# Four-layer graph network on one core: another order in layer 1's sort, table loop and last pass, and other places for chunk loads

## The chip, the core and the metric

The kernel runs on one core of one Trainium2 chip. The core's engines are TensorE (PE, matrix products into PSUM; the loading of its weights is shown apart as PEld), VectorE (DVE), ScalarE (ACT) and GpSimd (POOL). Data move between DRAM and the on-chip memory by DMA. Here the queue of SyncE (SP) issues the plain loads and stores, POOL's queue issues the indirect ones (gathers and scatters by row number), and a few come from ACT's queue. Each queue runs in order.

The metric is the device time of one execution in microseconds (us). Before the change it is 1217.2 us, the median of three runs (1211.95, 1217.2, 1225.6).

## The reference, cut to what matters

`x` is 2708 x 128 and `adj` is 2708 x 2708, both float32. Four layers run one after the other, each on `h = max(layernorm(x), 0)` with a residual sum. The change touches layer 1 and the aggregation that ends it:

```python
def _L1_gnn_ref(X, A, W, a):
    XW = jnp.matmul(X, W)
    s_col = jnp.matmul(XW, a[0, :f])
    s_row = jnp.matmul(XW, a[0, f:])
    Z1 = jax.nn.leaky_relu(s_row[:, None] + s_col[None, :], negative_slope=0.01)
    den = jnp.exp(Z1)
    num = jnp.matmul(A, den)
    att = jnp.where(num != 0, den / jnp.where(num != 0, num, 1.0), 0.0)
    H = jnp.matmul(A, jnp.matmul(att, XW))
    return H
...
h = jnp.maximum(_layernorm(x, axis=-1), 0.0)
x = x + _L1_gnn_ref(h, adj, L1_gnn_W, L1_gnn_a)
```

Layers 0, 2 and 3 each need a product of the whole of `adj` with 128 features as well; layer 0 also needs the four nearest neighbours of every node.

## The kernel before, in words

`adj` comes in transposed, so row k of it in DRAM is column k of `A`. It is cut into T = 22 **chunks** of 128 rows (1.354 MB each); the last chunk, number 21, has only 20 rows. The 2708 columns are cut into six blocks of at most 512, one PSUM bank each (`acc(0)` to `acc(5)`; two more banks, `ps_s`, serve short products in turn). On chip, chunks lie in `big` (four buffers), in five or six `res` buffers, or, for two of them, in the `lay` buffers with tags "Y" and "U", which other large tiles use at other times.

**Layer 1 without the big product.** `num` would be a 2708 x 2708 x 2708 product. But exp(leaky_relu(s_row + s_col)) is one of two products of exponentials, and which one holds for node k and column j depends only on whether s_row[k] lies above -s_col[j]. So the kernel sorts the nodes by s_row, builds a table with one row for each place in the sorted order (a *knot*), and finds every column of `num` by interpolating between two neighbouring rows of it. The stages are:

- *Sort (lines 748 to 883).* For t = 0 to 21, `place(t)` compares all nodes with the 128 of tile t: a mask on DVE (L779), its sum on ACT (L780), and counts on PE (L757). After every fourth tile `places_of` (L788) turns the counts into sorted places: a copy on DVE (L793), small products on PE (L797), `to_u` on DVE (L809), and then one scatter for each tile from POOL's queue (L814), which writes node number and s_row to `order_d` in DRAM. In between, `total(x_)` (L839) multiplies one chunk after the other, in 16 small products on PE (L847), into `tot`, the weighted total of all rows. Nine chunks are on chip already (`here`); thirteen more are loaded on SP's queue by `total_chunk` (L826, L836). The thirteen, n = 0 to 12, go to "Y", "U", then the four `big` buffers, and from n = 6 on to the five row buffers in turn. `total` is called at t = 1 to 11 and at even t from 12, one chunk a time, and what is left after the loop. `node_terms` (L857, a few small operations on PE, DVE and ACT for the columns' own terms) runs at t = 14.
- *Start of the table (L938 to L1005).* The sorted list is read back (`srtT`, L938), transposed on PE and turned into row numbers `src_u` (L943) and values `rs` (L944). `fetch(t)` (L946) gathers 126 rows of `adj` in sorted order into a `big` buffer (L950). The totals are moved into row 1 of the first of these tiles (L966, two DMAs from ACT's queue and two from SP's). Then `wt`, a 128 x 128 triangle of weights for every tile, is made: 44 matmul instructions on PE in six groups into `acc(1)` to `acc(5)` (L988), and 22 Relu operations on ACT (L999).
- *Table loop (L1030 to L1052).* For t = 0 to 21: the gather for t + 3 is issued, six products `wt[t]` x rows (L1036) give 128 knots, rows 0 and 1 are carried into the next tile on DVE (L1040), the knots are copied out on ACT and DVE (L1041) and stored to the table in DRAM on SP's queue (L1050, L1052). ACT also forms one row of signs (L908) a turn, four tiles ahead; `row_places` (L1016), at t = 19, finds from the signs which two table rows each column needs (`lo_u`, `hi_u`). Every third turn holds a group of XW (`node_product`, L1047).
- *Last pass (L1149 to L1158).* For each of the 22 tiles of 128 columns: gather the rows `lo` and `hi` (L1073), seven operations on single columns (L1094 to L1104), the interpolation on DVE (L1119), Ln and Exp on ACT (L1123, L1124), the product with `den` on DVE (L1131), and six products with XW on PE that add up in `py` (L1141). Tiles 0 to 3 are handled one by one and the others in pairs (`sets`); tile t is weighted (L1131, L1141) after tile t + 1 is interpolated. Tiles 0, 20 and 21 are split into two halves (`parts_of`). `lo` has four buffers, those of `big`; `hi` has six.
- *Aggregation (`aggregate`, L256).* `H` = A x (att XW): chunks 0 to 15 pass through the four `big` buffers, and chunks 16 to 21 are loaded into `res` buffers that stay for layers 2 and 3. In program order the load of `res` chunk 16 + i // 2 stands after chunk i for odd i: 0, 1, 16, 2, 3, 17, and so on. Chunk 21 is loaded four times, to four groups of 20 partitions. `aggregate` does the products of chunks 0 to 15 first, those of 16 to 21 at the end, and `res` buffers exist only once the last pass has left its `hi` buffers.

Program order sets the order of instructions marked `pin` only; the others on an engine may be moved by the scheduler that builds the program.

## Time and profile before

The profiled execution took 1218.29 us by its own clock; its span, from first to last instruction, is 1216.2 us, at a mean granted TensorE clock of 0.928. Stage by stage, from the busy time of each engine in stretches of the span:

| stretch, us | what runs | PE busy | DVE busy | ACT busy | POOL busy | DMA, GB/s |
|---|---|---|---|---|---|---|
| 484 to 537 | sort, totals | 46.86 | 33.46 | 36.24 | 24.20 | 290 |
| 537 to 700 | weights, table loop | 130.92 | 100.39 | 102.50 | 23.11 | 356 |
| 700 to 728 | start of last pass | 0.00 | 10.08 | 9.19 | 10.02 | 342 |
| 728 to 865 | last pass | 102.98 | 129.48 | 105.06 | 81.47 | 389 |
| 865 to 888 | its end, evacuation | 22.43 | 15.30 | 7.14 | 0.00 | 85 |
| 888 to 970 | aggregation, chunks 0 to 15 | 76.88 | 1.19 | 0.00 | 1.62 | 357 |
| 970 to 1000 | its end, next layer's start | 30.00 | 13.28 | 10.12 | 0.00 | 55 |

The stretches before 484 us are layer 0, those after 1000 us layers 2 and 3. A busy engine need not be the one that sets the pace, and an engine can be on the path while it is little busy; which wait ends last in each stretch has to be read from the single instructions. In the timeline each line has the start and the length in us, the engine, the line of the program, the operation with its operands, the number of merged instructions, and in brackets how long the engine had been idle before it and what it then waited for.

### The profile page before, as it was taken

What the parts mean: (1) busy time and instruction counts of PE and PEld (TensorE: products, weight loads), DVE (VectorE), ACT (ScalarE), POOL (GpSimd) and SP (SyncE); (2) the same over time, 40 slices, a digit from 0 to 9 for tenths busy, and PEclk for the clock granted to TensorE, in tenths of its full rate; (3) what the DMA queues carried; (4) which work ended last, traced back from release to release, by engine and by line L of the source; (5) the groups of instructions that cost most, each with busy time, mean ns of one, the idle gap of its engine ahead of it and who ended that gap; (6) DMA issues with size and microseconds to landing.
All of it is one profiled execution on the core that took longest, in us unless ns stands there. A gap on an engine that the chain in (4) does not pass through costs nothing.

```text
span 1216.2 us, 10253 instructions
## 1 busy us (share of the span) xinstructions
PE 1054.7 (87%) x3637; PEld 507.0 (42%) x3637; DVE 563.8 (46%) x1172; ACT 407.5 (34%) x643; POOL 237.0 (19%) x200
## 2 busy tenths in 40 slices
PE   4889999999969996977787807777999999999998
PEld 0325444444424445543333303333454455545444
DVE  2001004899972357816666648999720040114003
ACT  3100003444430034767667436878600040003000
POOL 0200000000017773441111035866000000000000
PEclk8998999999989996978989857998889999999999
DMA  8997830000059823869999889999299807753831
GB/s 307 426 359 299 307 133 1 1 0 1 1 218 400 318 53 113 360 222 322 367 380 403 350 351 418 424 424 380 82 383 351 317 33 276 268 184 105 308 136 46
DMA packets 40160, 298.77 MB, mean 246 GB/s; under 512 B 7103, under 2 KB 11214, under 8 KB 13650
## 3 DMA queue, kind: packets, MB, share of 16 engines
q1 hardware_dynamic: 24076, 202.37, 44.3%
q0 software_dynamic: 13600, 93.75, 20.3%
q10 hardware_dynamic: 2434, 2.01, 0.6%
q8 instruction: 29, 0.48, 0.2%
q14 instruction: 21, 0.17, 0.0%
HBM read 265.76 MB, written 32.87 MB: 246 GB/s over the span
## 4 chain that ended last, share of the span: by engine, by line
PE 53%; DVE 20%; DMA 19%; issue 6%; POOL 1%; ACT 1%; SPq 0%; POOLq 0%; DVEq 0%; ACTq 0%
PE acc L267 40%; DMA mov<-in_adj_dram,src_u 7%; DVE top_v L474 5%; DMA chunk<-in_adj_dram 5%; DVE top_i L476 5%; DVE hi L1131 4%; DVE hi L1119 4%; DMA hi<-table,hi_u 2%; DMA res<-in_adj_dram 2%; PE ps L847 2%; PE acc L1036 2%; PE acc L1141 1%; PE ps L224 1%; DMA xs<-in_x_dram 1%; PE ps L355 1%
## 5 line engine op out<-in xcount | busy, mean ns | idle before, releaser
L1141 PE MATMUL acc<-hi,xw 128*128 128x512 f32 (+2 forms) x264 | 119.8, 612 | 63.2 <-DVE hi L1131 63.2
L267 PE MATMUL acc<-chunk,y 128*128 128x512 f32 (+1 forms) x408 | 159.3, 554 | 12.8 <-DVE y L518 10.7
L267 PE MATMUL acc<-chunk,h 128*128 128x512 f32 (+1 forms) x384 | 148.0, 542 | 0.0
L1036 PE MATMUL acc<-mov,wt 128*128 128x512 f32 (+1 forms) x264 | 119.7, 608 | 28.7 <-DMA mov<-in_adj_dram,src_u 28.7
L539 POOL DMA_INDIRECT gath<-ydr,near_u x88 | 84.4, 959 | 284.8 <-DMA ydr<-y 258.3
L267 PEld LDWEIGHTS acc<-chunk,y 128*128 128x128 f32 x408 | 75.0, 194 | 97.1 <-issue 85.6
L463 PE MATMUL acc<-zT 128*128 128x512 f32 (+2 forms) x264 | 108.2, 552 | 1.5 <-ACT strip L472 1.1
L1141 PEld LDWEIGHTS acc<-hi,xw 128*128 128x128 f32 (+1 forms) x264 | 53.7, 212 | 129.1 <-DVE hi L1131 66.7
L1040 DVE COPY mov<-acc 2x512 f32<-2x512 f32 (+1 forms) x126 | 74.6, 612 | 61.0 <-PE acc L1036 59.6
L267 PEld LDWEIGHTS acc<-chunk,h 128*128 128x128 f32 x384 | 68.8, 190 | 74.1 <-issue 74.1
L1036 PEld LDWEIGHTS acc<-mov,wt 128*128 128x128 f32 x264 | 52.5, 210 | 92.0 <-issue 78.0
L472 ACT COPY strip<-acc 128x512 f32<-128x512 f32 (+2 forms) x132 | 60.7, 558 | 73.5 <-issue 58.5
L267 PE MATMUL acc<-chunk,attended 128*128 128x512 f32 x192 | 76.9, 563 | 5.1 <-DMA chunk<-in_adj_dram 5.1
L463 PEld LDWEIGHTS acc<-zT 128*128 128x128 f32 (+1 forms) x264 | 46.4, 185 | 57.3 <-issue 34.1
L1073 POOL DMA_INDIRECT lo<-table,lo_u x22 | 56.0, 2547 | 71.5 <-DVE hi L1119 31.5
L1041 ACT COPY knots<-acc 128x512 f32<-128x512 f32 x88 | 49.9, 586 | 55.7 <-DVE mov L1040 40.0
L1119 DVE SCALAR_TENSOR_TENSOR hi<-lo,lam,hi 128x2708 f32<-128x2708 f32 (+4 forms) x25 | 67.2, 2697 | 1.0
L1123 ACT ACTIVATE hi<-hi,lam 128x2708 f32<-128x2708 f32 (+4 forms) x25 | 56.7, 2280 | 32.5 <-issue 23.4
L1131 DVE SCALAR_TENSOR_TENSOR hi<-row_all,inv_s,hi 128x2708 f32<-128x2708 f32 (+4 forms) x25 | 67.0, 2692 | 0.0
L474 DVE MAX8 top_v<-strip 128x8 f32<-128x2708 f32 (+1 forms) x22 | 64.3, 2963 | 0.2 <-ACT strip L472 0.2
L476 DVE FIND_INDEX8 top_i<-top_v,strip 128x8 uint32<-128x2708 f32 x20 | 59.2, 2972 | 0.0
L545 DVE SCALAR_TENSOR_TENSOR xs<-gath,simd,xs 128x128 f32<-128x128 f32 (+1 forms) x88 | 30.6, 351 | 59.9 <-DMA gath<-ydr,near_u 59.2
(270 smaller groups left out, 1168.1 us busy)
## 6 DMA issues: line engine op xcount, KB each, us to landing
chunk<-in_adj_dram SPq DMA_DIRECT2D x110, 1354.0 KB
table<-knots SPq DMA_DIRECT2D x20, 1354.5 KB
res<-in_adj_dram SPq DMA_DIRECT2D x9, 1354.0 KB
res<-in_adj_dram SPq DMA_DIRECT2D x8, 211.6 KB
ydr<-y SPq DMA_DIRECT2D x2, 704.0 KB
gath<-ydr,near_u POOLq DMA_INDIRECT x88, 5.5
chunkY<-in_adj_dram SPq DMA_DIRECT2D x1, 1354.0 KB
chunkU<-in_adj_dram SPq DMA_DIRECT2D x1, 1354.0 KB
```

The costliest lines, as they stand in the source:

```text
L267: nc.tensor.matmul(out[b][:, :n], y[r, i, :], chunk(i)[r, k0 : k0 + n], start=(i == 0), stop=(i == T - 2),)
L463: mm = nc.tensor.matmul(zz[b][:w, :n], zT[:, cols(t)], zT[:, k0 : k0 + n], start=True, stop=False)
L472: nc.scalar.copy(s[:w, k0 : k0 + n], zz[b][:w, :n])
L474: nc.vector.max(top_v[:w, t, :], s[:w, :])
L476: nc.vector.max_index(top_i[:w, t, :], top_v[:w, t, :], s[:w, :])
L539: nc.gpsimd.indirect_dma_start(out=g[:w, :], out_offset=None, in_=ydr[:, :], in_offset=bass.IndirectOffsetOnAxis(ap=near_u[:w, t, k : k + ...
L1036: nc.tensor.matmul(p[:, :n], wt[:, t, :], moving[t][:, k0 : k0 + n], start=True, stop=True)
L1040: nc.vector.tensor_copy(moving[t + 1][:2, k0 : k0 + n], p[:2, :n])
L1119: nc.vector.scalar_tensor_tensor(num, lo[:w, c], kap, num, op0=ALU.mult, op1=ALU.add)
L1123: nc.scalar.activation(num, num, AF.Ln, scale=sc)
L1131: nc.vector.scalar_tensor_tensor(att[:w, c], row_all[:w, c], inv_s[:w, t : t + 1], att[:w, c], op0=ALU.max, op1=ALU.mult,)
L1141: nc.tensor.matmul(py[b][:, :n], xw[:w, t, :], att[:w, k0 : k0 + n], start=(t == 0), stop=(t == T - 1),)
```

## The change

There are five parts. (1) *Sort:* the last two chunk loads, n = 11 and 12, go to "U" and "Y" instead of the row buffers; `total` is called at t = 1 to 13 and at 15, 16, 18 and 20; `node_terms` runs at t = 16. (2) *Start of the table:* the first three gathers are issued right after `src_u`, ahead of `rs` and the totals; the four DMAs of the totals all go on SP's queue. (3) *Table loop:* the weights are made in groups of four tiles, the first before the loop and group t // 4 + 1 at the end of turn t for t = 0, 4, 8, 12, 16, in the `ps_s` banks; `row_places` runs at t = 18. (4) *Last pass:* tile 21, the one of 20 columns, is first, alone and not split; then 0, 1, 2 alone, and the pairs (3, 4) to (19, 20). (5) *Aggregation of layer 1:* `back=3` puts the loads of the `res` chunks two chunks later: 0, 1, 2, 3, 16, 4, 5, 17, and so on, with 21 after 13. The other aggregations keep their order (`back=1`).

```diff
-    def aggregate(y, done, more=None, kept=0):
+    def aggregate(y, done, more=None, kept=0, back=1):
...
-            if i % 2 and last + i // 2 < T:
-                chunk(last + i // 2)
+            j = last + (i - back) // 2
+            if i >= back and (i - back) % 2 == 0 and j < T:
+                chunk(j)
...
-        if n < 2:
-            c = lay.tile([P, N], F32, name="chunk" + "YU"[n], tag="YU"[n])
+        if n < 2 or n > 10:
+            tag = "YU"[n % 2]
+            c = lay.tile([P, N], F32, name="chunk" + tag, tag=tag)
...
-        if t == 14:
+        if t == 16:
             node_terms()
-        if 1 <= t <= len(here) + 2 or t % 2 == 0 and t:
+        if 1 <= t <= len(here) + 4 or t in (15, 16, 18, 20):
             total(done)
...
     nc.vector.tensor_copy(src_u[:PER, :], p[:PER, :T])
-    nc.vector.tensor_copy(rs, p[:, T : 2 * T])
...
+    for t in range(3):
+        fetch(t)
+    nc.vector.tensor_copy(rs, p[:, T : 2 * T])
...
-        (nc.scalar, nc.sync)[g % 2].dma_start(
+        nc.sync.dma_start(
             first[1:2, QUARTER * g : QUARTER * (g + 1)], tots[32 * g : 32 * g + 1, :]
         )
-    for t in range(3):
-        fetch(t)
...
-    for t0, t1 in GROUPS:
-        p = acc(1 + t0 // 4 % 5)
+
+    def weights(g):
+        t0, t1 = GROUPS[g]
+        p = ps_s.tile([P, 512], F32, name="ps")
...
+
+    weights(0)
...
-        if t == T - 3:
+        if t == T - 4:
             row_places()
+        if t % 4 == 0 and t // 4 + 1 < NG:
+            weights(t // 4 + 1)
...
-        return [slice(0, HALF), slice(HALF, N)] if t < 1 or t >= T - 2 else [slice(0, N)]
+        return [slice(0, HALF), slice(HALF, N)] if t in (0, T - 2) else [slice(0, N)]
...
-                start=(t == 0),
-                stop=(t == T - 1),
-            )
-
-    sets = [(t,) for t in range(4)] + [(t, t + 1) for t in range(4, T, 2)]
+                start=(t == T - 1),
+                stop=(t == T - 2),
+            )
+
+
+    sets = [(T - 1,)] + [(t,) for t in range(3)] + [(t, t + 1) for t in range(3, T - 1, 2)]
...
-            if t:
-                weighed(t - 1)
-    weighed(T - 1)
+            if before:
+                weighed(before.pop())
+            before.append(t)
+    weighed(before.pop())
...
-    aggregate(attended, to_h2, ahead(lambda g: node_product(yT, None, g, attend), 1))
+    aggregate(attended, to_h2, ahead(lambda g: node_product(yT, None, g, attend), 1), back=3)
```

## The prediction

> **What bounds the kernel now.** I read the chain of waits first: no engine bounds the whole span, so I took layer 1 stage by stage, from the timeline of each engine and the busy time in stretches. There are four places where something other than the busiest engine ends a wait.

> *The end of the sort.* First the chain of waits, then POOL's timeline:

> ```profile
> 525.49 8.28 DMA chunk<-in_adj_dram
> 533.82 2.48 PE ps L847 x16
> ```
> ```profile
> 528.23 0.89 POOL L814 DMA_INDIRECT order_d<-pay,to_u  x1 [0.30 <-issue]
> 534.25 0.59 POOL L938 DMA_DIRECT2D srtT<-order_d  x1 [5.14 <-DMA order_d<-pay,to_u]
> 537.81 1.10 POOL L950 DMA_INDIRECT mov<-in_adj_dram,src_u  x1 [2.97 <-DVE pw L979]
> ```

> Two strands end together near 536: the last chunk, issued at 525.49 only because a row buffer came free late, and the last scatter, for which POOL idles 5.14. The first gather starts at 537.81.

> *The table loop.* PE's timeline:

> ```profile
> 552.37 4.78 PE L1036 MATMUL acc<-mov,wt 128*128 128x512 f32 x12 [1.36 <-DMA mov<-in_adj_dram,src_u]
> 559.31 6.48 PE L1036 MATMUL acc<-mov,wt 128*128 128x512 f32 x12 [2.16 <-DMA mov<-in_adj_dram,src_u]
> ...
> 694.08 4.78 PE L1036 MATMUL acc<-mov,wt 128*128 128x512 f32 x12 [0.90 <-DMA mov<-in_adj_dram,src_u]
> ```

> Turns 1, 2 and 21 start when their gathers land: (694.08 - 552.37) / 20 = 7.09 a gather. The first interval is 6.94, most of it before the first table store at 554.35: the stream of gathers sets the pace, not PE, ACT or the stores.

> *The start of the last pass.* DVE's timeline:

> ```profile
> 716.46 0.21 DVE L1094 TENSOR_SCALAR lam<-hi,lo 128x1 f32<-128x1 f32 x1 [3.25 <-DMA hi<-table,hi_u]
> ...
> 749.50 0.21 DVE L1094 TENSOR_SCALAR lam<-hi,lo 128x1 f32<-128x1 f32 x1 [3.08 <-DMA hi<-table,hi_u]
> ...
> 750.75 3.04 DVE L1119 SCALAR_TENSOR_TENSOR hi<-lo,lam,hi 128x2708 f32<-128x2708 f32 x1
> ```

> `hi` of tile 0 lands at 716.4, of tile 5 at 749.4: 6.6 a tile, so the stream began at 709.8. From 750.75 DVE has no gap to the end; a pair takes 13.39 (777.74 - 764.35).

> *The aggregation.* PE's timeline:

> ```profile
> 888.04 51.98 PE L267 MATMUL acc<-chunk,attended 128*128 128x512 f32 x132
> 942.32 6.51 PE L267 MATMUL acc<-chunk,attended 128*128 128x512 f32 x12 [2.29 <-DMA chunk<-in_adj_dram]
> 951.65 18.44 PE L267 MATMUL acc<-chunk,attended 128*128 128x512 f32 x48 [2.83 <-DMA chunk<-in_adj_dram]
> ```

> PE waits twice for chunks. From 970 to 1180 it is busy without a gap, so what is won before arrives at the end in full.

> [...] while chunk 21's four 20-row loads were in flight (934 to 942) the engines moved 135 to 184 GB/s, against some 420 otherwise. [...] the read of the sorted list took 2.0, the quickest scatter 2.1.

> **Part 1 and 2, sort and start.** "U" and "Y" are free by 509.9 (the last product that reads U), so loads 11 and 12 are issued near 510 instead of 523.27 and 525.49. The nine before them fill the DMA until about 520.9; two at 3.2 (1.354 MB at 420 GB/s) end near 527.3, not 531.6, and the last totals near 532 instead of 536.3. Then the scatters decide. Up to `places_of(3)` the count of totals stays thirteen and `node_terms` is gone (about 1.0 of PE; its DVE operations add up to 1.6): tiles 12 to 15 may go about 1 sooner. From there to `places_of(4)` PE gains one total (16 products, 1.25) and `node_terms` (1.0). So `to_u` of tiles 16 to 19, at 520.78 now, comes 0.5 to 2.4 later; POOL, which reaches them at 521.87, is held about 0.9. Six scatters of 1.27 follow: the last starts near 529.1. Beside a quiet DMA it needs 2.1 to 2.6, not 5.4: the sorted list is read at about 531.9, 2.3 sooner. The gather now waits for `src_u` (done at 536.90) and not for DVE work to 537.71; scatters start 0.27 after `to_u`, so 0.6 is won. Sum 2.9; I take **2.5**, bounds -1.5 (all of the 2.4, no quicker landing) and 4.5. The four total DMAs on SP cost 4 x 0.6 there, SP being empty; they are needed at gather 0's landing, 7.3 after its issue. Three gathers move ahead on POOL (1.05 + 0.3 each), past nothing.

> **Part 3, table loop: 0.** The 44 instructions of L988 (539.21 to 546.46) leave the front. Gather 0 landed at 545.1, so PE was 1.2 late; it had caught up before turn 1, where it waits 1.36. In the loop, five turns get 8 x 0.165 = 1.3 of PE and 4 x 0.36 = 1.5 of ACT. A turn of 7.09 has 5.4 of PE (38.03 of 50 busy, 600 to 650) and 4.6 of ACT (32.56 of 50). Behind the groups stand the next turn's products and copies; a late product would delay only the gather four tiles on, and three are in flight, 14 us of cover. Should ACT run late, the copies out of `acc` hold PE: rival C. `row_places` (eleven DVE operations, 3.3) moves off turn 20, where it ran beside the copies from 689.47 to 696.28; the last turn began with its gather and copied rows were there in time: 0, and DVE idles 3.76 where it goes. Its last sign row comes from turn 17, in time. Bounds -1 to +1.

> **Part 4, last pass.** The first pair is now (3, 4): before it come 0.43 MB and five tiles instead of six. [...] `hi` of tile 4 lands at 709.8 + 3.2 + 33.0 = 746.0, not 749.4: **3.4** sooner. DVE is ready by then: tile 21 (1.25 of small operations, 3.04, 3.03), 0 (7.6, split), 1 (7.3) and 2 (4.3) are 26.5 of work from 713 on. Buffers: `lo` of 3 needs tile 21's interpolation, near 717, long before its data. Afterwards two tiles of stream, 13.2, stay just under DVE's 13.39. Tail: now tiles 20 and 21 are weighted back to back, and PE runs from 864.23 to 881.80 behind DVE, 23.7 after the last pair's first operation. Then it is (19, 20), eight pairs after 747.3, at 854.4; tile 19 is weighted by 866.4, and two tiles of PE at 5.3 end at 877.0: 4.8 in all, 5.0 with tile 21's two halves gone. I take **5.0**, bounds 2 and 7.

> **Part 5, aggregation.** Sixteen chunks take 82.05. Two waits are 5.1, and the 6.51 against 4.61 (18.44 / 4), PE's clock having fallen to 0.5, is 1.9: 7.0 to win. Now chunks 2 and 3 stand behind `res` 16 on SP, which waits for the last pass (881.83); then they go ahead while the DMA idles (85 GB/s, 865 to 888), two loads or 6.4 of head start. At 3.2 a load, chunk 11 then lands 45 after PE's start and is needed at 52; chunk 13, with the slow 20-row loads behind it, lands at 59 to 61 and is needed at 61. I take **5.8**, bounds 2.5 and 8.

> **Sum.** 2.5 + 5.0 + 5.8 = 13.3. The profiled execution's own 1218.3 becomes 1205.0; it stood 1.1 above the median of 1217.2, so I predict 1204.

> **Rivals.**
> *A, the start wins nothing and the last pass little:* the extra total holds the scatters, and the short gathers cost 4. For it: PE is busy 28.4 of the 30 us from 490 to 520. Against: the DMA is free at its end. Left: 0 + 1 + 5.8, about 1210.
> *B, the aggregation's wait only moves:* the 20-row loads now stand before chunks 14 and 15. For it: the DMA is full from 890 to 950. Against: the head start equals the wait. 0.5 there instead of 5.8: 1209.
> *C, slower:* the groups in the loop are paid serially. In five turns 1.3 of PE, 1.5 of ACT and the 2.74 sign row ahead of it stand before the next copies: 5.5, less the 1.7 that a turn has free, 3.8 x 5 = 19; less 13.3, about 1223. It decides if PE regains under 3.8 in the three turns after a group, and a chain of PE and ACT replaces the gathers as pace. Against: landings stayed at 7.1 after PE's longest turns.
> *D, the scheduler puts the unpinned work elsewhere,* all groups before the loop as now: about 1205, counted with the forecast.

> **Chances.** Forecast (with D) 0.66, A 0.14, B 0.14, C 0.06. 1% of 1217.2 is 12.2, about what a measurement tells from no change; the forecast lies at that edge (1205.0), somewhat more of it below. Faster by over 1%: 0.66 x 0.75 and a little of B, 0.52; slower C, 0.06; within 0.42. Taken together, the bounds reach 1197 to 1215; with A and B, 8 in 10 lie in 1196 to 1212.

> **What would show it.** First gather near 535.3 (right) or at 537 and later (part 1 wrong). Gathers still 7.1 apart, else part 3 is wrong. The first pair's interpolation 41 us after the first `lo` issue instead of 44.5 (750.75 - 706.22). Chunk waits on PE in the aggregation under 2. The forecast fails if the loop's turn exceeds 7.3 or a 20-row gather takes over 4.

## The result, and the profile after

The change makes the kernel faster by a little under half of what I forecast: 1213.39 us against 1219.72 (medians of 20 runs each). The ratio, estimated from the single runs, is 0.9951 with a 95% interval of 0.993 to 0.9973. That is 6.0 us (3.3 to 8.5 at the interval's ends); the forecast was 13.3. Single runs of either kernel lie up to 8 us from their median. Of all runs below one, with part 5 alone, took 2721.59 and is left out. The profiled execution of the changed kernel took 1207.17 (span 1205.5), 6.2 under its median, while that of the kernel before lay 1.4 under its own. So the two traces differ by 11.1, and the trace alone would have confirmed me. What follows is read with that in mind.

The line numbers have moved a little: the scatters L814 are L816, `srtT` L938 is L941, the gathers L950 are L952, `lam` L1094 is L1103, the interpolation L1119 is L1128, and the aggregation's products L267 are L268. POOL's timeline at the end of the sort:

```profile
528.87 0.90 POOL L816 DMA_INDIRECT order_d<-pay,to_u  x1 [0.30 <-issue]
533.06 0.58 POOL L941 DMA_DIRECT2D srtT<-order_d  x1 [3.30 <-DMA order_d<-pay,to_u]
536.50 1.10 POOL L952 DMA_INDIRECT mov<-in_adj_dram,src_u  x1 [2.86 <-DVE tots L969]
```

The last scatter starts at 528.87, before at 528.23. But layer 0 happened to take 1.56 longer in this execution (first scatter at 496.43, before at 494.87), so the scatters took 0.9 less, where I had put them 0.9 later. The last one also lands sooner: POOL idles 3.30 for it, not 5.14. From the first scatter on, the first gather comes 40.1 later; it was 42.9. DVE's timeline has the row numbers that the gather needs, first in this trace and then in that of the kernel before:

```profile
535.41 0.18 DVE L946 CAST src_u<-acc 126x22 uint32<-126x22 f32 x1 [0.67 <-PE acc L944]
```
```profile
536.72 0.18 DVE L943 CAST src_u<-acc 126x22 uint32<-126x22 f32 x1 [0.49 <-PE acc L941]
```

The gather starts 0.91 after they are done in both (536.50 and 537.81), so moving it ahead on POOL won nothing by itself. PE's timeline in the table loop, turns 1 and 19:

```profile
552.46 4.71 PE L1043 MATMUL acc<-mov,wt 128*128 128x512 f32 x12
...
681.08 13.65 PE L1043 MATMUL acc<-mov,wt 128*128 128x512 f32 x30 [2.86 <-DMA mov<-in_adj_dram,src_u]
```

That is 128.62 / 18 = 7.15 a turn, with gathers still the pace; it was 7.09. DVE's timeline in the last pass, its first pair and its last one:

```profile
744.99 0.21 DVE L1103 TENSOR_SCALAR lam<-hi,lo 128x1 f32<-128x1 f32 x1 [3.07 <-DMA hi<-table,hi_u]
...
746.24 3.04 DVE L1128 SCALAR_TENSOR_TENSOR hi<-lo,lam,hi 128x2708 f32<-128x2708 f32 x1
...
839.94 3.04 DVE L1128 SCALAR_TENSOR_TENSOR hi<-lo,lam,hi 128x2708 f32<-128x2708 f32 x1
...
853.87 0.21 DVE L1103 TENSOR_SCALAR lam<-hi,lo 128x1 f32<-128x1 f32 x1 [1.78 <-DMA hi<-table,hi_u]
...
855.20 3.04 DVE L1128 SCALAR_TENSOR_TENSOR hi<-lo,lam,hi 128x2708 f32<-128x2708 f32 x1
```

The first pair starts at 746.24, 41.8 after the first `lo` issue (704.40). The pairs then follow at 13.39, but the last one comes 15.26 after the one before it: DVE waits for `hi`. I had not foreseen that wait; it is on the chain of waits, as is one chunk of the aggregation (start, length, what):

```profile
839.56 14.29 DMA hi<-table,hi_u
...
933.12 16.78 DMA chunk<-in_adj_dram
```

PE's timeline in the aggregation:

```profile
882.95 63.77 PE L268 MATMUL acc<-chunk,attended 128*128 128x512 f32 x168
949.95 9.35 PE L268 MATMUL acc<-chunk,attended 128*128 128x512 f32 x24 [3.23 <-DMA chunk<-in_adj_dram]
959.23 4.32 PE L268 MATMUL acc<-res,attended 20*128 20x512 f32 x17
```

One wait is left, of 3.23, after 168 products, which is at chunk 14 (168 / 12). The sixteen chunks take 76.3 instead of 82.0. But the same program, profiled again (the third of three traces of it), shows this:

```profile
880.86 63.77 PE L268 MATMUL acc<-chunk,attended 128*128 128x512 f32 x168
950.60 12.34 PE L268 MATMUL acc<-chunk,attended 128*128 128x512 f32 x24 [5.96 <-DMA chunk<-in_adj_dram]
962.87 3.46 PE L268 MATMUL acc<-res,attended 20*128 20x512 f32 x15
```

The wait is 5.96 here, and the 24 products after it take 12.34 instead of 9.35: 82.0 in all, nothing won in this execution. So the first trace can't be taken as the rule.

### The profile page after: what moved, and what is told of

Same layout as the page of the kernel before. It is cut to its first block, busy times and chain, and to the rows that moved or that the text cites. A ratio compares the mean times of both kernels' runs of the same rounds, so it can differ in the third digit from the quotient of the medians.

```text
span 1205.5 us, 10245 instructions
## 1 busy us (share of the span) xinstructions
PE 1049.8 (87%) x3637; PEld 504.7 (42%) x3637; DVE 563.1 (47%) x1170; ACT 407.5 (34%) x641; POOL 240.0 (20%) x200
## 5 line engine op out<-in xcount | busy, mean ns | idle before, releaser
L1150 PE MATMUL acc<-hi,xw 128*128 128x512 f32 (+3 forms) x264 | 122.5, 625 | 58.1 <-DVE hi L1140 58.1
L268 PE MATMUL acc<-chunk,y 128*128 128x512 f32 (+1 forms) x408 | 160.4, 556 | 12.8 <-ACT y L518 10.6
L268 PE MATMUL acc<-chunk,h 128*128 128x512 f32 (+1 forms) x384 | 148.0, 542 | 0.0
L268 PEld LDWEIGHTS acc<-chunk,y 128*128 128x128 f32 x408 | 75.3, 195 | 97.9 <-issue 86.4
L1047 DVE COPY mov<-acc 2x512 f32<-2x512 f32 x126 | 74.1, 611 | 59.6 <-PE acc L1043 59.2
L268 PEld LDWEIGHTS acc<-chunk,h 128*128 128x128 f32 x384 | 68.8, 190 | 74.1 <-issue 74.1
L268 PE MATMUL acc<-chunk,attended 128*128 128x512 f32 x192 | 73.1, 542 | 3.2 <-DMA chunk<-in_adj_dram 3.2
L1132 ACT ACTIVATE hi<-hi,lam 128x2708 f32<-128x2708 f32 (+3 forms) x24 | 56.5, 2362 | 35.5 <-issue 26.6
L1128 DVE SCALAR_TENSOR_TENSOR hi<-lo,lam,hi 128x2708 f32<-128x2708 f32 (+3 forms) x24 | 67.0, 2800 | 1.0
L1140 DVE SCALAR_TENSOR_TENSOR hi<-row_all,inv_s,hi 128x2708 f32<-128x2708 f32 (+3 forms) x24 | 67.0, 2797 | 0.4 <-ACT hi L1133 0.4
```

Source lines behind the costliest of these rows:

```text
L268: nc.tensor.matmul(out[b][:, :n], y[r, i, :], chunk(i)[r, k0 : k0 + n], start=(i == 0), stop=(i == T - 2),)
L1047: nc.vector.tensor_copy(moving[t + 1][:2, k0 : k0 + n], p[:2, :n])
L1128: nc.vector.scalar_tensor_tensor(num, lo[:w, c], kap, num, op0=ALU.mult, op1=ALU.add)
L1132: nc.scalar.activation(num, num, AF.Ln, scale=sc)
L1140: nc.vector.scalar_tensor_tensor(att[:w, c], row_all[:w, c], inv_s[:w, t : t + 1], att[:w, c], op0=ALU.max, op1=ALU.mult,)
L1150: nc.tensor.matmul(py[b][:, :n], xw[:w, t, :], att[:w, k0 : k0 + n], start=(t == T - 1), stop=(t == T - 2),)
```

## The experiments

All ratios are to the kernel before, timed beside each kernel on the same chip; they are estimated from the single runs and are not the quotients of the two medians. Most medians are of 11 to 22 runs; the last four rows have six or seven each. When the four kernels with a single part were timed, all of them, and the kernel before beside them, took some 90 longer, about 80 of it ahead of the sort (first scatter at 573.5 to 578.1). Why is open; what is compared there is each against 1309.57. "Loop" is from the first gather to the first `lo` issue, "stage" from the first `lo` issue to the first product with `res` (last pass and sixteen chunks), both from each kernel's one profiled execution. From the first product with `res` to the end every trace takes 246.2 to 246.5, so what is won before does arrive in full, as I had assumed.

| kernel | median / before | ratio (95%) | first scatter to first gather | loop | stage | waits for chunks |
|---|---|---|---|---|---|---|
| before, first trace | – | – | 42.9 | 168.4 | 263.8 | 5.1 |
| before, again | 1218.55 / 1219.33 | 0.9984 (0.9965–1.0003) | 42.6 | 173.9 | 259.1 | 4.6 |
| parts 1, 2 alone | 1304.11 / 1309.57 | 0.9959 (0.9938–0.998) | 45.4 | 170.7 | 259.2 | 4.8 |
| part 3 alone | 1309.57 / 1309.57 | 1.0003 (0.9983–1.0024) | 51.2 | 170.6 | 260.4 | 3.4 |
| part 4 alone | 1307.7 / 1309.57 | 0.9985 (0.9964–1.0005) | 53.4 | 170.8 | 258.3 | 5.9 |
| part 5 alone | 1309.88 / 1309.57 | 0.9998 (0.9969–1.0028) | 53.4 | 171.0 | 264.5 | 4.7 |
| the change | 1213.39 / 1219.72 | 0.9951 (0.993–0.9973) | 40.1 | 167.9 | 254.8 | 3.2 |
| the change, second | 1213.94 / 1219.96 | 0.9957 (0.9935–0.998) | 39.0 | 169.2 | 253.0 | 2.3 |
| the change, third | 1210.91 / 1219.33 | 0.9936 (0.9908–0.9964) | 39.7 | 168.5 | 260.5 | 6.0 |
| without 5 | 1215.21 / 1219.96 | 0.9958 (0.9938–0.9978) | 39.5 | 173.8 | 258.4 | 5.5 |
| without 5, again | 1213.2 / 1219.33 | 0.9959 (0.9936–0.9983) | 40.2 | 167.9 | 259.7 | 5.4 |
| without 4 | 1217.92 / 1219.03 | 0.9988 (0.9964–1.0013) | 39.1 | 167.5 | 264.0 | 4.6 |
| without 3 | 1214.31 / 1219.03 | 0.9955 (0.9933–0.9977) | 39.3 | 170.0 | 253.2 | 2.6 |
| without 1, 2 | 1218.6 / 1219.03 | 0.9999 (0.9979–1.0019) | 43.0 | 171.4 | 255.4 | 3.4 |
| res 16, 17 ahead | 1212.82 / 1219.03 | 0.9953 (0.9936–0.997) | 39.9 | 174.4 | 260.4 | 4.6 |
| res 21, 16 ahead | 1205.28 / 1219.96 | 0.9914 (0.9882–0.9946) | 39.7 | 168.6 | 248.8 | 0 |
| res 21 first, old places | 1208.42 / 1220.5 | 0.9907 (0.9875–0.9938) | 39.0 | 169.5 | 253.2 | 2.1 |
| chunk 0 held | 1205.68 / 1220.5 | 0.9891 (0.9852–0.993) | 39.9 | 170.4 | 252.0 | 3.9 |
| res 21 ahead, chunk 0 held | 1204.14 / 1219.96 | 0.9876 (0.9828–0.9924) | 39.2 | 174.6 | 246.4 | 0 |
| the same, again | 1203.47 / 1219.33 | 0.9864 (0.9822–0.9907) | 39.1 | 170.6 | 246.4 | 0 |

### Each part alone

Each of the four is the kernel before with the hunks of one part of the change's diff; the lines that carry them:

```diff
 parts 1 and 2
+        if n < 2 or n > 10:
+        if 1 <= t <= len(here) + 4 or t in (15, 16, 18, 20):
+    for t in range(3):
+        fetch(t)
 part 3
+        if t % 4 == 0 and t // 4 + 1 < NG:
+            weights(t // 4 + 1)
 part 4
+    sets = [(T - 1,)] + [(t,) for t in range(3)] + [(t, t + 1) for t in range(3, T - 1, 2)]
 part 5
+    aggregate(attended, to_h2, ahead(lambda g: node_product(yT, None, g, attend), 1), back=3)
```

Parts 1 and 2: 

> Parts 1 and 2 alone (loads 11 and 12 in Y and U, node_terms at 16, totals' schedule, three gathers ahead of the totals); the weights, the last pass and the aggregation are those of before. Theory S (every part gains in the median what the two traces show; the shortfall is a chance of the profiled run): first gather 40.1 after the first scatter (before 42.9), median 2.5 to 3 under before. Theory R (the gain is given back later, because the table loop or the last pass is set by transfers that don't start sooner): the same first gather, but the median within 1. Rival: the last scatters vary in landing and the gain is there in this trace only by chance: first gather at 42 or later after the first scatter.

Part 3: 

> Part 3 alone (weights by groups in the loop, row_places at T - 4). Theory S: 0, within 1 of before, gathers still 7.1 apart, loop from first to last product as long as before (152.6). Theory W (the groups cost the loop time in most executions, and the profiled one hid it): 3 to 6 slower in the median.

Part 4: 

> Part 4 alone (tile of 20 columns first in the last pass). Theory S: end of the products into py 2.5 to 5 sooner after the first lo issue than before (175.6), median 2 to 4.5 under before. With the old order of the aggregation's loads, chunks 0 and 1 alone are ahead of the end of the pass, so theory P (the chunk loads of the new order delay the last hi gather) expects the whole 5.0 here, the last pair at 149 after the first lo issue. Theory L (the pass gains nothing in the median): within 1.

Part 5: 

> Part 5 alone (back=3). Theory S: the first sixteen chunks in 76.3 instead of 82.0, median 5 to 6 under before. Theory P (loads of chunks 2 and 3 go ahead during the last hi gathers and delay them): the end of py 1 to 2 later, median 3.5 to 4.5 under before. Theory B (the wait only moves, in most executions): 0 to 2.

The sort takes longer in these four, and 42.9 doesn't hold there: without parts 1 and 2 the first gather comes 51.2 to 53.4 after the first scatter, with them 45.4. The median gains 5.5. Part 3 is nothing, as forecast. Part 4 gains 1.9, with an interval that includes zero, and "the whole 5.0" of theory P is refuted: its last pair is late too (14.9 after the one before), with only chunks 0 and 1 loading. Part 5 gains nothing. Its PE timeline:

```profile
985.24 65.41 PE L268 MATMUL acc<-chunk,attended 128*128 128x512 f32 x168
1055.33 11.76 PE L268 MATMUL acc<-chunk,attended 128*128 128x512 f32 x24 [4.68 <-DMA chunk<-in_adj_dram]
```

Two waits of before, 5.1 in sum (4.6 in one wait at chunk 12 in the second trace of that kernel), have become one of 4.68, and it stands at chunk 14, as in the changed kernel. This is my rival B.

### Where the wait of the aggregation comes from

SP's queue in the first trace of the changed kernel (start and length, the length including waits for a buffer), and the busy time in stretches (columns: PE, PEld, DVE, ACT, POOL, granted clock, DMA share, GB/s):

```profile
877.89 0.33 SPq L245 DMA_DIRECT2D res<-in_adj_dram  x1
887.69 4.87 SPq L245 DMA_DIRECT2D chunk<-in_adj_dram  x2
892.61 0.42 SPq L245 DMA_DIRECT2D res<-in_adj_dram  x1
896.77 4.87 SPq L245 DMA_DIRECT2D chunk<-in_adj_dram  x2
...
928.96 1.47 SPq L245 DMA_DIRECT2D res<-in_adj_dram  x4
933.12 26.54 SPq L245 DMA_DIRECT2D chunk<-in_adj_dram  x6
```

```profile
883.00:888.00 5.00, 5.00 (x16) 2.37 (x15) 1.10 (x5) 0.00 (x0) 1.61 (x3) 1.00 0.03 6
...
929.00:934.00 5.00, 5.00 (x14) 2.35 (x14) 0.00 (x0) 0.00 (x0) 0.00 (x0) 1.00 1.03 433
...
939.00:944.00 5.00, 5.00 (x14) 2.34 (x13) 0.00 (x0) 0.00 (x0) 0.00 (x0) 1.00 1.00 193
```

Two things stand out. The DMA idles from 883 to 888 (6 GB/s): behind `res` 16 stands chunk 4, which needs the buffer of chunk 0, and `res` 17 stands behind that. And from 929 on the four 20-row loads of `res` 21 run through the full stream: 193 GB/s instead of 433. The chunk issued behind them at 933.12 lands at 949.9. Which of the two is the cause? `res` 16 and 17 ahead of chunk 4 fills the idle DMA; `res` 21 and 16 there fills it too and takes the 20-row loads out of the stream; `res` 21 first with the old places does only the latter.

```diff
+    LATER = {3: (T - 6, T - 5), 5: (T - 4,), 7: (T - 3,), 9: (T - 2,), 11: (T - 1,)}
...
-            j = last + (i - back) // 2
-            if i >= back and (i - back) % 2 == 0 and j < T:
-                chunk(j)
+            if back == 1 and i % 2 and last + i // 2 < T:
+                chunk(last + i // 2)
+            if back == 3 and i in LATER:
+                for j in LATER[i]:
+                    chunk(j)
```

With `res` 21 and 16 ahead, and with `res` 21 first in the old places, the first line is

```diff
+    LATER = {3: (T - 1, T - 6), 5: (T - 5,), 7: (T - 4,), 9: (T - 3,), 11: (T - 2,)}
+    LATER = {1: (T - 1,), 3: (T - 6,), 5: (T - 5,), 7: (T - 4,), 9: (T - 3,), 11: (T - 2,)}
```

The change once more: 

> The change as it is, once more, on the chip that the next three share. Theory D (with back=3 only one res load can go ahead of chunk 4, since the second stands behind chunk 4's wait for a buffer; the DMA idles until PE's start and the head start is given back): DMA under 50 GB/s in the first 5 us of the aggregation, one wait of 3 to 6 for a chunk, median 5 to 7 under before. Rival B2 (22 loads with the slow 20-row ones can't come in time, whatever the order): the same here; the runs with the order changed tell them apart.

Without part 5 (`back=1`): 

> The change without part 5 (back=1). My forecast of part 5: 5.8 slower than the change. Theory D: within 2 of the change, waits for chunks of 3 to 6 in sum as with it.

Res 21 and 16 ahead: 

> The change, with the loads of res 21 (the 20-row ones) and res 16 ahead of chunk 4, where the DMA idles, the others two chunks sooner each. Theory D: no wait for a chunk, sixteen chunks in 73 to 74, median 3 to 6 under the change. Rival B2: a wait of 3 or more stays, median within 1.5 of the change.

Res 16 and 17 ahead: 

> The change, with res 16 and res 17 ahead of chunk 4 and the others two chunks sooner each; res 21 with its 20-row loads stays the last. This is the head start of two loads that I had counted on. Theory D (the idle DMA is all that is wrong): waits for chunks under 1 in sum, sixteen chunks in 73 to 74, as with res 21 ahead. Rival D2 (the 20-row loads must move too): a wait of 2 or more in the middle of the aggregation, median 0 to 2 under the change.

Res 21 first, old places: 

> The change with part 5's places taken back (a res load after every odd chunk from 1 on, as in the kernel before), but with res 21 first and 16 to 20 after it. Theory Q (the place of the 20-row loads alone makes the wait): no wait for a chunk or under 1, sixteen chunks in 73 to 75, median within 3 of the run with res 21 ahead and back=3 (1205), so 7 to 9 under the change. Rival H (the head start is needed too): the chunks 2 and 3 behind the 20-row loads come late: a wait of 2 to 5 early in the aggregation, median within 3 of the change.

Theory D falls. With `res` 16 and 17 ahead the DMA is in use early, and still PE waits, two chunks sooner, since the 20-row loads now come two chunks sooner:

```profile
889.04 54.69 PE L270 MATMUL acc<-chunk,attended 128*128 128x512 f32 x144
948.30 21.22 PE L270 MATMUL acc<-chunk,attended 128*128 128x512 f32 x48 [4.57 <-DMA chunk<-in_adj_dram]
```

With `res` 21 ahead there is no wait at all; PE runs 192 products in one piece, and the 20-row loads run where the DMA idled (139 GB/s from 876 to 881):

```profile
876.24 72.86 PE L270 MATMUL acc<-chunk,attended 128*128 128x512 f32 x192
949.03 4.32 PE L270 MATMUL acc<-res,attended 20*128 20x512 f32 x17
```

```profile
876.00:881.00 5.00, 5.00 (x15) 2.57 (x16) 1.39 (x6) 0.00 (x0) 1.60 (x3) 1.00 0.94 139
```

The median falls by 8.7 against the change beside it; the ratio falls from 0.9957 to 0.9914, which is 5.2, and the two intervals just overlap. With the old places and `res` 21 first, most of that stays (1208.42, ratio 0.9907): five waits of 0.3 to 0.5, 2.1 in sum, and sixteen chunks in 76.4, more than theory Q allowed, but no wait after which PE is slower. So the place of the 20-row loads makes the long wait, and the head start of part 5 is the smaller matter. Whether it is the slow rate of these loads or that they are four was not tried. The head start can't be kept anyway: SP issues two chunks every 9.08 (887.69, 896.77), PE's own pace (63.77 / 14 = 4.56 a chunk), since each load waits for the buffer that PE has just left.

### The late last pair

The first chunk's load was held by an order on DVE: a write of one element into its buffer stands behind the last pair's factors, and the load behind that. The chunk's data overwrite the element.

```diff
         interpolation(ts)
+        if ts == sets[-1]:
+            c = resident[0] = big.tile([P, N + 1], F32, name="chunk", tag="big")
+            pin(nc.vector.memset(c[0:1, 0:1], 0.0))
+            pin(nc.sync.dma_start(c[:, :N], adjT[:P, :]))
```

With `res` 21 and 16 ahead as well: 

> As the run with res 21 ahead, and chunk 0 (with it all loads behind it on SP) held until the last pair's factors have been computed. Theory P (chunk loads that start 12 us before the last hi gather has landed delay it): last pair's interpolation 13.4 after the pair before it instead of 15.3, end of py 1.5 to 2 sooner, median 1 to 2.5 under the run with res 21 ahead, since the chunks are there in time anyway. Rival P2 (the stream of gathers itself is as slow as that): last pair as before, median within 1.

Alone, on the change: 

> The change, with chunk 0's load alone held until the last pair's factors have been computed; res 21 stays last. Theory P (the first chunk loads delay the last hi gather): last pair 13.4 after the pair before it, end of py 170.1 after the first lo issue instead of 172.9; the wait for a chunk in the middle of the aggregation stays at 2 to 6, so the median is 1 to 4 under the change. If the early loads were of use for the aggregation, it would be within 1 of the change.

In the eleven traces with part 4 and without the hold the last pair comes 14.8 to 16.3 after the one before it; in the three with the hold, 13.4. DVE's timeline of the last pair and the one before it, from the second trace of the kernel with both edits:

```profile
845.33 3.04 DVE L1132 SCALAR_TENSOR_TENSOR hi<-lo,lam,hi 128x2708 f32<-128x2708 f32 x1
...
858.72 3.04 DVE L1132 SCALAR_TENSOR_TENSOR hi<-lo,lam,hi 128x2708 f32<-128x2708 f32 x1
```

So the loads of chunks 0 and 1, which in the changed kernel are issued at 843.01 and 848.91 while the last gathers (issued at 836.61 and 839.56) are under way, do delay them; chunks 2 and 3 follow only when these have landed. That fits part 4 alone, which had just these two loads there and its last pair late as well. The hold does a second thing that I had not meant. PE's timeline of the same kernel, after the last products into `py`:

```profile
879.98 1.04 PE L222 MATMUL ps<-ident,yT 128*128 128x128 f32 x8
881.02 4.81 PE L270 MATMUL acc<-chunk,attended 128*128 128x512 f32 x12
885.67 0.60 PE L222 MATMUL ps<-ident,yT 128*128 128x128 f32 x4
886.10 13.80 PE L270 MATMUL acc<-chunk,attended 128*128 128x512 f32 x36
```

The scheduler now puts the first chunks' products between the transposes (L222), so PE's first product follows the end of `py` by 0.9 instead of 5.1. Of these 4.2, 2.6 are given back, since the transposes now stand within the sixteen chunks (75.4 instead of 72.8 with `res` 21 ahead). Alone the hold brings the ratio to 0.9891 (six runs), against 0.9936 to 0.9957 for the change: 5 to 8 us, about twice what I gave it. The earlier products may be the reason, but how much each of the two effects is worth was not tried apart. On top of `res` 21 ahead the hold takes 1.1 off the median, 4.6 by the ratios. The two edits together give 1203.47 and 1204.14, 15.8 under the kernel before: the best version here, and 7.4 and 9.8 under the change beside it, where I expected 8 to 11.

### Each part taken away, and the traces again

Each of these is the change with one part's hunks taken back, so the diffs above with the signs turned.

Without part 4: 

> The change without part 4 (old order of the last pass). My forecast: 5.0 slower than the change. By the stages of the traces so far: first pair's interpolation 44.9 after the first lo issue instead of 41.3, PE's first product of the aggregation 4.2 later, and the loads of the aggregation start less well (chunk 4 is issued 12.6 after the end of py instead of 9.8): 4 to 7 slower. Rival (part 4 alone gained 1.9 in the median): 1 to 2.5 slower.

Without part 3: 

> The change without part 3 (all weights before the loop, row_places at T - 3). Forecast: within 1 of the change. Rival W: the groups cost the loop 1 to 3, so 1 to 3 faster than the change, and first gather to first lo issue under 170 instead of 170.8 (mean of six traces).

Without parts 1 and 2: 

> The change without parts 1 and 2. By the traces the first gather comes 39.5 after the first scatter with them (mean of five) and 42.9 without (the kernel before): 3 to 3.5 slower than the change if the start passes on to the end in full. Rival: the table loop, which lasts 152.6 to 158.8 from run to run, absorbs it: within 1.5.

Without part 4 the change keeps 1.1 of its gain, with 264.0 in the stage: there the first product waits longer after `py` (6.2 instead of 5.1), and the DMA idles longer with it (6 GB/s from 885.5 to 890.5), so part 5 without part 4 probably loses what it might win; that wasn't tried apart. Without part 3 nothing moves. Without parts 1 and 2 nothing is left of the gain, within 2.6 either way.

The last four runs were to settle why the medians gave half of what the traces showed (for the kernel before, the change, the change without part 5, and the best version):

> The kernel before once more. If the favourable traces of the change were chance: first lo issue to first res product within 259 to 264, as in the traces so far, and a profiled time within 4 of its median. If profiled executions are favourable in themselves: a profiled time 4 or more under its median, here too.

> The change once more. Chance: first lo issue to first res product now over 255 and the profiled time within 4 of the median of 1213 to 1214. Theory V (parts 4 and 5 do gain 7 in this stage, and another stage, the table loop, is longer in most timed runs than in the profiled ones): the stage at 253 to 255 again, the loop from first gather to first lo issue over 170.

> The change without part 5 once more. Theory V: first lo issue to first res product at 258, and the median 3 to 5 over the change. Theory B (the wait only moves): median within 2 of the change.

> Res 21 and 16 ahead of chunk 4, and chunk 0 held until the last pair's factors. If the aggregation's waits and the late last pair are what kept the change from its forecast: no wait for a chunk, last pair 13.4 after the one before, median 8 to 11 under the change.

The third trace of the change has its stage at 260.5, as long as in the kernel before (259.1 and 263.8) and no shorter than without part 5 (258.4, 259.7). Theory V falls, and chance had a large share. That it was chance alone isn't shown: of the five traces with parts 4 and 5 and the loads in the order of the change, four have the sixteen chunks in 75.3 to 76.4 and one in 82.0, and the three with part 4 and the old order have them in 80.9 to 81.3, while the timed runs of the change without part 5 are only 1.3 and 2.3 above those with it. The profiled times of the four are 4.8 over, equal to, 2.6 under and 1.0 over their medians; in all twenty traces they lie from 11.9 under to 5.3 over, thirteen of them under.

The rest of the trace scatters as much as the gain. The four kernels with a single part left out, the first scatter, which no part changes, comes at 490.4 to 500.3, and the loop takes 167.5 to 174.6 in kernels of either kind. Without these two stretches, that is from the first scatter to the first gather and in the stage, the two traces of the kernel before take 306.7 and 301.7 and the three of the change 294.9, 292.0 and 300.2: 8.5 less in the means, where the timed runs give 6.0 (3.3 to 8.5).

## Why the prediction was wrong, step by step

**Part 5 failed, and it is the step that broke the sum.** I put 5.8; the runs give nothing alone and 1.3 to 2.3 with the rest, neither clear of the scatter. Two steps were wrong. The "two loads or 6.4 of head start", chunks 2 and 3 (not `res` 16 and 17, as I wrote ahead of that run), did go ahead (issued at 858.26 and 864.29, before at 882.21), but nothing could follow them: with the four buffers full, chunk 4 waits on SP until PE has done chunk 0, `res` 17 stands behind it, and the DMA idled for the 5 us from 883 to 888. And I followed the loads only to chunk 13, "needed at 61", as if the 20-row loads behind it were then harmless; chunks 14 and 15 stand behind those. Rival B said just that, and I set it aside with "the head start equals the wait". The slow loads were in my own working: 8 us at less than half the rate put the stream back by some 4 to 5 (an estimate from the 161 and 200 GB/s of the slowest 8 us in the first traces of the two kernels, where the stream has 417 to 433), and with the idle stretch filled (`res` 16 and 17 ahead) a wait of 4.57 was left. The traces show that these four loads are slow; why isn't shown.

I had also counted 1.9 of lost clock as certain to come back. With the wait at chunk 14 it comes back only when the wait is short: after 2.3 to 3.4 the 24 products took 9.35, after 4.6 to 6.0 they took 11.8 to 12.3. That makes the aggregation either some 76 or some 82, and the first trace showed the good case.

**Part 4 was mis-sized: 5.0 forecast.** Its first step held: the first pair comes at 40.7 to 42.3 after the first `lo` issue, forecast 41.1 (without it 44.5 to 45.4). The 3.2 in it for the two short gathers was an estimate of mine that no trace showed. The trace of before puts it only between 2.5 and 4: the next `lo` is issued 2.54 after the first, and the four 20-row loads were in flight for the 8 us from 934 to 942, two in half of that. The first trace of the change has 3.9: `hi` of the first full tile is there 14.13 after the first `lo` issue (718.53 - 704.40), before 10.24 (716.46 - 706.22). The step "two tiles of stream, 13.2, stay just under DVE's 13.39" holds between the first eight pairs and fails for the last, where chunk loads share the DMA: 1.4 to 3.0 lost. The end of `py` comes 172.8 after the first `lo` issue instead of 175.1 (means of eleven and six traces), so 2.3 is won, and 1.1 more as the first product then follows sooner. With chunk 0 held it comes after 170.0 (mean of three), 5.1 sooner: the size I had given, so the delay by the chunk loads is what I had left out. In timed runs part 4 is worth 1.9 alone and 4 to 6 in the whole.

**Parts 1 and 2 were too small, and their sum was not the right one.** Forecast 2.5; the first gather is 3.4 sooner (42.9 in three traces, 39.5 in thirteen with the parts, the four kernels with a single part left out). The quicker landing was right: the sorted list is read 3.1 to 4.2 after the last scatter starts, without the parts 5.7 to 6.1. But the scatters, which I had put 0.9 later, end 1.0 sooner (the last starts 32.4 after the first, before 33.4), and the 0.6 of a gather freed from DVE work isn't there: it starts 0.9 after `src_u` is done in all twenty traces. That 2.5 came near was in part luck. Timed runs give 5.5 alone and 5 to 8 in the whole, more than the 3.4; why isn't settled.

**Part 3 was right:** 0 within the interval, alone and taken away; the loop is as long with it as without (167.5 to 174.6 and 168.4 to 173.9). Rival C, the only way to a loss, is out. Rival D is out too: in the first trace the six groups run at 536.8, 551.6, 578.9, 604.1, 639.8 and 662.4, so inside the loop. Rival A is out with the start.

The forecast's base was low as well: I worked from a median of three runs, 1217.2, where it is 1219 to 1220. The likeliest case without part 5 (rival B, 8.0 off) would have stood inside the interval of 3.3 to 8.5.

## What to carry to other kernels

When a stream of loads fills the DMA behind a few buffers (here 417 to 433 GB/s behind four), look first for the transfer in it that runs slower than the others, and move that to where the DMA idles; loading the others earlier gained little here, since the buffers paid out loads at the consumer's pace (two chunks every 9.08, PE's 4.56 a chunk). Follow every load behind a moved one to the consumer that needs it, not to the first that comes in time. And before one profiled execution is taken as a measure of a gain of 1%, profile the same program twice more: here a stage that looked 9 shorter was 11 shorter in the second trace and 3 in the third.

## What the runs showed of the hardware

A wait of PE for a chunk can be dearer than its length. After waits of 4.57 to 5.96 (nine traces) the next 24 or 48 products take 1.4 to 3.0 longer; the granted clock, read in six of the nine, is then 0.5 for about 3.4 or 6.8 us. After 2.25 to 3.37 (four traces of the changed kernel and its relatives) they take no longer. Between these the length doesn't tell: 1.7 longer after 3.42 and after 3.89, and in the kernel before 1.9 longer after 2.29 and no longer after 2.83.

```profile
939.53:942.94 3.41, 1.12 (x5) 0.58 (x4) 0.00 (x0) 0.00 (x0) 0.00 (x0) 1.00 0.94 149
942.94:946.36 3.42, 3.42 (x6) 1.36 (x5) 0.00 (x0) 0.00 (x0) 0.00 (x0) 0.50 0.97 355
```
```profile
945.26:948.67 3.41, 1.46 (x5) 0.57 (x3) 0.00 (x0) 0.00 (x0) 0.00 (x0) 1.00 0.96 353
948.67:952.08 3.41, 2.13 (x5) 1.06 (x6) 0.00 (x0) 0.00 (x0) 0.00 (x0) 1.00 0.99 419
```

PE idles 0.67 of the first stretch, and the clock falls at its end; in the longer wait it idles at most 0.57 of a stretch, and the clock stays. Of the seventeen waits of over 1 us twelve are followed by slower products and five are not. For twelve of the seventeen the stretches can be read (for nine of these from stretches of 4 us, which give the share of idle time to a few hundredths). In nine the products are slower: the first wait of the kernel before, the four kernels with a single part, the third trace of the change, the first without part 5, `res` 16 and 17 ahead, and chunk 0 held. There PE idles for 0.60 or more of the stretch at whose end the clock falls to 0.5; the 0.60 is that of chunk 0 held. In three they are not: the second wait of the kernel before and those in the first two traces of the change. There PE idles for at most 0.57 of any stretch, and the clock stays at 1.00. What sets the grid isn't shown.

While the four 20-row loads run, the DMA moves less. In the first trace of the kernel before the slowest 8 us after their issue move 161 GB/s (934 to 942), in that of the change 200 (937.6 to 945.6), after a stream of 417 (897 to 929) and 433 (929 to 934). With `res` 21 ahead they run before the stream, at 139 from 876 to 881. In the fifteen traces read in stretches of 4 us the slowest stretch with these loads moves 133 to 203. The loads queued behind them are kept back: the chunk issued at 933.12 in the first trace of the change took 16.8 to land.
